# Attention and mixture-of-experts layer on one core: keys of a block turned by transposing DMAs, and the block cut into eight steps

## The chip, the cores and the metric

The kernel runs on one core of a Trainium2 chip. A core has a matrix engine (TensorE, PE in the profile; its weight loads are PEld), a vector engine (VectorE, DVE), a scalar engine (ScalarE, ACT), GpSimd (POOL) and a queue engine (SyncE, SP) that issues DMAs; 16 DMA engines move data between HBM and the on-chip memory SBUF, or within SBUF. Matmuls write to PSUM. The engines run side by side, each through its own instructions in order, and wait for one another on semaphores. The metric is device time in microseconds of one execution, as a median over runs.

## The reference

An input x of 8 sequences of 1024 tokens with 256 features is normalised (layer norm without gain) to xn, and two branches are added to x:

```python
q, k, v = (xn @ W.T).reshape(B, L, 16, 16)         # 16 heads of 16
q, k = elu(q) + 1, elu(k) + 1
kv_cumsum = cumsum(einsum('blhd,blhe->blhde', k, v), axis=1)
k_cumsum  = cumsum(k, axis=1)
out   = einsum('blhd,blhde->blhe', q, kv_cumsum)
denom = clip(einsum('blhd,blhd->blh', q, k_cumsum), 1e-6)
attn  = (out / denom).reshape(B, L, 256) @ Wo.T

logits = xn @ Wr + br                              # 8 experts, the best two per token
h   = silu(xn @ W1[e]) * (xn @ W3[e])              # 256 -> 512
ffn = sum over the two of weight * (h @ W2[e])     # 512 -> 256
result = x + attn + ffn
```

All of it is float32.

## The kernel before

**Two streams of work.** The FFN branch gathers tokens by expert into tiles of 128 rows. Tiles j = 0 to 131 are worked off in a loop (`tile_step`, L1397); each needs the expert's W1 and W3 (two DMAs of 512 KB from SP, `ffn_weights`, L1284, issued for tile j + 2 in step j into a ring of five buffers), 32 matmul records into `gu_ps` (L1310), a silu on ACT (L1318), a product `hT` on DVE (L1321), 8 matmul records into `y_ps` (L1329, for the tile before) and a scaling `y` on DVE (L1336), and a scattering DMA from POOL (L1340). The tiles 0 to 24 come from a first batch of lists, the others from a second, whose lists are made in tiles 12 to 21 (`second_batch`, L719: pieces of a one-hot on DVE, scalings on ACT, matmuls `held_ps` on PE).

The attention branch goes through 16 blocks of 512 tokens, two to a sequence, as a chain of steps (`block_steps`, L1032). It is linear attention in chunks of 128 tokens with a running state per head. A block t has nine steps:

1. q for both halves of the heads (`project_q`, elu, and masked copies qm by ACT, L829)
2. k of all four chunks (`project_k`, L841; elu by ACT, table load included, L786 and L787, and DVE, L789), with tokens on the partitions (`kn`)
3. k turned, so that features are on the partitions (`kT`): for each half of the heads four PE transposes (L882) and an ACT copy from PSUM (L885); then on DVE a running sum over the tokens (`ksum`, L887), its last column kept for the next block (`upto_t`, L891), and the product with q (L892)
4. v (`project_v`, four ACT copies L852) and the denominators: matmuls `den` (L904) from both products, clip and reciprocal on DVE (L910, L911), and eight DMAs from SP that spread the result (`rden`, L916)
5. the fetch of the next block's turned xn, the scores of chunk 0 (`scores`, L928: PE L936, causal mask on DVE L943), and the output projection left over from the block before (`attend`, L1008)
6. to 9. one chunk each: `carry` (L955), scores of the next chunk, `weigh` (L973, L983; DVE L990, L993, L1002), and the projection of the chunk before.

**What sets the order.** In the main loop PE's instructions stand in the order in which the code issues them (`manual_schedule`, L1480). In a tile that is: attention's step or steps, gu of this tile, y of the tile before. The order on ACT, DVE and POOL is a planner's, except for instructions under `in_order`, which keep the program's order among themselves; SP's DMAs are all of that kind. How many attention steps have been made by tile j is a table (`upto`, L1456 to L1461); `attend_upto` (L1072) makes one step per tile, or two where the second is in `TOGETHER`, and may put a block's last step behind gu. The first ones of block 0 are made before the loop, with transposes on PE.

**Turning by DMA** is there already for the FFN: from tile 27 on the gathered rows xg are split by DVE into planes of their low and high 16-bit halves (`ffn_halves`, L1241), turned by a transposing DMA of two-byte elements (`ffn_turn_halves`, L1250, on SP between the two weight loads), and put together again by an ACT copy that interleaves the halves (`ffn_join`, L1259). Tiles before 27 are turned by PE (L1269, copy L1271).

**Buffers.** Pool `one` holds one buffer each of qT, qm, kn, kT and rden; `f_x` holds five buffers of 4 KB per partition for blocks of x, loaded for blocks 4 to 15; `ps_mm` is a ring of four PSUM banks shared by gu, projections and scores, `ps_y` one of two shared by y, den and a.

Of the kernel before, what the change touches and what calls it, by code (L numbers as in the profile page):

```python
# [46 lines left out]
F32 = mybir.dt.float32  # L47
I32 = mybir.dt.int32
BF16 = mybir.dt.bfloat16
U16 = mybir.dt.uint16  # L50
AF = mybir.ActivationFunctionType
ALU = mybir.AluOpType
AX = mybir.AxisListType

P = 128
# [9 lines left out]
def tile_attention_moe(  # L65
# [14 lines left out]
    nc = tc.nc  # L80
# [727 lines left out]
    def begin(t):  # L808
        names = dict(
            qT=[KC, TB], qm=[KC, 2, TB], kn=[NCH, H], kT=[KC, TB], rden=[NCH, KC, P]  # L810
        )
        tiles = {n: one.tile([P, *d], F32, tag=n, name=n) for n, d in names.items()}
        blocks[t] = tiles["qT"], tiles["qm"], tiles["kT"], tiles["kn"], va, tiles["rden"]
# [34 lines left out]
    def project_v(t, c):  # L848
# [6 lines left out]
            )  # L855
        yield

    def project(t):


        if t > 0:
            begin(t)
            for o in range(KC):
                for _ in project_q(t, o):
                    pass
                mask_q(t, o)
                yield
            for c in range(0, NCH, 2):
                for _ in project_k(t, c):
                    pass  # L870
                yield
        else:
            for _ in range(4):
                yield
        qT, qm, kT, kn, va, rden = blocks[t]
        upto_t = two.tile([P, KC], F32, tag="upto_t", name="upto_t")
        fresh = t % BLK_PER_SEQ == 0
        qks = []
        for o in range(KC):
            tp = ps_t.tile([P, TB], F32, tag="t", name="tp")  # L880
            for c in range(NCH):
                nc.tensor.transpose(  # L882
                    tp[:, bass.ts(c, P)], kn[:, c, bass.ts(o, P)], ident
                )
            nc.scalar.copy(kT[:, o, :], tp)  # L885
            ksum = two.tile([P, TB], F32, tag="ksum", name="ksum")
            nc.vector.tensor_tensor_scan(  # L887
                ksum, ones[:, 0:1].to_broadcast([P, TB]), kT[:, o, :],
                0.0 if fresh else sums[0][:, o : o + 1], ALU.mult, ALU.add,
            )  # L890
            nc.vector.tensor_copy(upto_t[:, o : o + 1], ksum[:, TB - 1 : TB])  # L891
            nc.vector.tensor_tensor(ksum, qT[:, o, :], ksum, ALU.mult)  # L892
            qks.append(ksum)
            yield
        for c in range(0, NCH, 2):
            if t > 0:
                for _ in project_v(t, c):
                    pass
            yield

        den = ps_y.tile([P, P], F32, tag="y", name="den")
        for o in range(KC):
            for c in range(NCH):
                nc.tensor.matmul(  # L904
                    den[32 * c : 32 * c + 32, :], lhsT=own_of[:, o, :],
                    rhs=qks[o][:, bass.ts(c, P)], start=(o == 0), stop=(o == KC - 1),
                    skip_group_check=True,
                )
        over = one.tile([P, P], F32, tag="over", name="over")
        nc.vector.tensor_scalar(over, den, EPS_DEN, None, ALU.max)  # L910
        last_masked[0] = nc.vector.reciprocal(over, over)  # L911
        for c in range(NCH):
            for o in range(KC):
                heads_of = slice(32 * c + HALF * o, 32 * c + HALF * (o + 1))
                in_order(
                    nc.sync.dma_start(  # L916
                        out=rden[:, c, o, :],
                        in_=over[heads_of, :].unsqueeze(1).to_broadcast([HALF, HD, P]),
                    )
                )  # L920
        yield
        del xnTs[t]
        sums[0] = upto_t

# [107 lines left out]
    def block_steps(t):  # L1032


        for i, _ in enumerate(project(t)):
            if i in (1, 3, 5, 8):
                yield
        if t + 1 < NBLK:
            fetch(t + 1)
        waiting = scores(t, 0)  # L1040
        if behind:
            attend(*behind.pop())
        yield
        done = None
        for c in range(NCH):
            if done:
                attend(*done)
            both_ps = carry(t, c)
            coming = scores(t, c + 1) if c + 1 < NCH else None
            oT = weigh(both_ps, *waiting)  # L1050
            done = t, c, oT
            waiting = coming
            yield
        behind.append(done)
        if t + 1 == NBLK:
            attend(*behind.pop())
            yield

    STEPS = 9
    LAST = NBLK * STEPS + 1  # L1060

    TOGETHER = (0, 4, 8)
    steps_made = [0]

    def attention():
# [325 lines left out]
    LATE = 3  # L1391
    LISTS = NBLK - FB
    READ = LISTS + 10
    AHEAD = 2 + LISTS // 2 + 3 * (READ - LISTS) // 2
    held = {}

    def tile_step(j):  # L1397
# [58 lines left out]
        if j < LISTS:  # L1456
            upto = 3 + j // 2
        elif j < READ:
            upto = AHEAD - 3 * (READ - j - 1) // 2
        else:  # L1460
            upto = AHEAD + (LAST - 1 - AHEAD) * (j - READ + 1) // (NM - 1 - READ) + j // (NM - 1)  # L1461
        waits = attend_upto(upto, put_off=True)
# [74 lines left out]
```

## Time and profile before

| | |
|---|---|
| median of 3 runs | 1265.2 us (1262.7 to 1265.59) |
| profiled execution | 1257.66 us, span 1255.5 us |
| PE busy | 1205.5 us, 96% |
| DVE, ACT, POOL busy | 675.3, 554.5, 527.9 us |
| transposes of k, L882 | 128 records, 273 ns median each, overlapping |
| copies of kT on ACT, L885 | 32, 586 ns median |
| key sums, L887 with a carried start | 16, 1266 ns median |
| transposing DMAs, L1250 | 105, issue 1227 ns median |
| joins of halves, L1259 | 105, 757 ns median |
| DMA in total | 245.84 MB, mean 196 GB/s |

A line of the timeline reads: start in us, length in us, engine, line of the kernel, operation, output<-input, shapes, number of instructions merged; in brackets the idle time of that engine before it and who ended it. Merged matmuls overlap, so what a group costs PE is read from its start to the next group's start. A line of the windows view gives a stretch, its length, the busy time of PE, PEld, DVE, ACT and POOL (instructions in brackets), the granted TensorE clock as a share of full speed, the DMA engines' mean busy share and GB/s.

### The profile page before, as it was taken

What the parts mean: (1) busy time and instruction counts of PE and PEld (TensorE: products, weight loads), DVE (VectorE), ACT (ScalarE), POOL (GpSimd) and SP (SyncE); (2) the same over time, 40 slices, a digit from 0 to 9 for tenths busy, and PEclk for the clock granted to TensorE, in tenths of its full rate; (3) what the DMA queues carried; (4) which work ended last, traced back from release to release, by engine and by line L of the source; (5) the groups of instructions that cost most, each with busy time, mean ns of one, the idle gap of its engine ahead of it and who ended that gap; (6) DMA issues with size and microseconds to landing.
All of it is one profiled execution on the core that took longest, in us unless ns stands there. A gap on an engine that the chain in (4) does not pass through costs nothing.

```text
span 1255.5 us, 29756 instructions
## 1 busy us (share of the span) xinstructions
PE 1205.5 (96%) x11460; PEld 1059.7 (84%) x11460; DVE 675.3 (54%) x1541; ACT 554.5 (44%) x1064; POOL 527.9 (42%) x460
## 2 busy tenths in 40 slices
PE   7788898999999999999999999999999999999994
PEld 5677787888888889888888889989888889898884
DVE  7776669975344544545453545445453545445451
ACT  5665454471624335262625335262626243352610
POOL 4733234325443544444434544444443354444322
PEclk8899999999999999999999999999999999999997
DMA  9788565747987887969888787979897987879672
GB/s 339 274 276 266 150 209 116 237 115 229 245 196 182 193 198 167 244 151 227 177 200 182 187 202 167 223 169 223 185 200 171 189 193 178 205 165 247 145 178 33
DMA packets 203934, 245.84 MB, mean 196 GB/s; under 512 B 72946, under 2 KB 127858, under 8 KB 203506
## 3 DMA queue, kind: packets, MB, share of 16 engines
q1 hardware_dynamic: 161010, 191.79, 52.9%
q0 software_dynamic: 38032, 43.22, 24.6%
q10 hardware_dynamic: 4752, 8.91, 2.0%
q8 instruction: 94, 1.54, 0.5%
q14 instruction: 46, 0.38, 0.1%
HBM read 187.91 MB, written 44.29 MB: 185 GB/s over the span
## 4 chain that ended last, share of the span: by engine, by line
PE 87%; DVE 7%; DMA 2%; ACT 2%; issue 1%; SPq 0%; POOL 0%; POOLq 0%; ACTq 0%; DVEq 0%
PE gu_ps L1310 36%; PE y_ps L1329 17%; PE s_ps L936 5%; PE o_ps L973 5%; PE a_ps L1015 5%; PE zq L819 4%; PE zkk L835 4%; PE zkv L835 4%; PE o_ps L955 2%; DMA xb<-in_x_dram 1%; PE tp L882 1%; PE held_ps L749 1%; PE tp L358 1%; PE den L904 1%; DVE st L312 1%
## 5 line engine op out<-in xcount | busy, mean ns | idle before, releaser
L1310 PE MATMUL gu_ps<-xgT,w 128*128 128x128 f32 x4224 | 504.6, 277 | 6.4 <-issue 2.9
L1310 PEld LDWEIGHTS gu_ps<-xgT,w 128*128 128x128 f32 x4224 | 487.3, 192 | 21.1 <-issue 12.7
L1340 POOL DMA_INDIRECT out_dram<-y,dst_i x107 | 175.4, 1639 | 320.2 <-DVE y L1336 96.8
L1329 PE MATMUL y_ps<-w_sb,hT 128*128 x1056 | 250.9, 380 | 2.1 <-DVE tab L327 1.1
L1218 POOL DMA_INDIRECT xg<-in_x_dram,src_i x132 | 129.0, 977 | 229.1 <-DVE half L1241 114.4
L1329 PEld LDWEIGHTS y_ps<-w_sb,hT 128*128 128x128 f32 x1056 | 190.5, 190 | 24.8 <-issue 1.6
L1318 ACT ACTIVATE hT<-gu_ps 128x512 f32<-128x512 f32 x132 | 78.8, 597 | 286.9 <-PE gu_ps L1310 237.4
L943 DVE TENSOR_TENSOR s_sb<-s_ps,causal 128x512 f32<-128x512 f32 x256 | 159.0, 681 | 70.5 <-PE s_ps L936 68.1
L1321 DVE TENSOR_TENSOR hT<-gu_ps,hT 128x512 f32<-128x512 f32 x132 | 90.3, 684 | 63.0 <-PE gu_ps L1310 28.2
L1223 POOL DMA_INDIRECT entry<-tab_d,of_i x107 | 107.2, 1002 | 39.5 <-issue 31.4
L1336 DVE TENSOR_SCALAR y<-y_ps,entry 128x256 f32<-128x256 f32 x132 | 63.7, 482 | 109.9 <-PE y_ps L1329 109.9
L1241 DVE COPY half<-xg 128x512 uint16<-128x512 uint16 x105 | 47.9, 457 | 130.7 <-ACT xg L1231 130.7
L1020 ACT COPY at<-a_ps 128x256 f32<-128x256 f32 x64 | 23.8, 373 | 173.0 <-PE a_ps L1015 123.0
L1259 ACT COPY xgT<-halfT 128x512 uint16<-128x512 uint16 x105 | 79.7, 759 | 5.1 <-DMA halfT<-half 5.1
L1231 ACT ACTIVATE xg<-xg,entry 128x256 f32<-128x256 f32 x132 | 78.4, 595 | 2.1 <-DMA entry<-tab_d,num_i 2.1
L936 PE MATMUL s_ps<-qm,kT 32*128 32x256 f32 x1024 | 75.3, 400 | 0.1
L1015 PE MATMUL a_ps<-wo_sb,oT 128*128 128x256 f32 x256 | 67.9, 388 | 2.9 <-DVE y L1336 2.0
L973 PE MATMUL o_ps<-s_sb,va 128*32 128x128 f32 x2048 | 69.2, 276 | 0.0
L973 PEld LDWEIGHTS o_ps<-s_sb,va 128*32 128x32 f32 x2048 | 52.0, 109 | 17.8 <-issue 15.9
L1340 POOL DMA_INDIRECT acc_d<-y,src_i x25 | 44.2, 1766 | 52.6 <-DVE y L1336 23.3
L835 PE MATMUL zkv<-wkv_sb,xnT 128*128 128x256 f32 x256 | 59.9, 388 | 0.0
L835 PE MATMUL zkk<-wkv_sb,xnT 128*128 128x256 f32 x256 | 59.4, 386 | 0.0
(228 smaller groups left out, 1339.1 us busy)
## 6 DMA issues: line engine op xcount, KB each, us to landing
w<-in_w_dram SPq DMA_DIRECT2D x264, 512.0 KB
rden<-over SPq DMA_DIRECT2D x128, 64.0 KB
xnT<-xnT_d SPq DMA_DIRECT2D x15, 512.0 KB
out_dram<-at POOLq DMA_DIRECT2D x13, 512.0 KB
out_dram<-in_x_dram SPq DMA_DIRECT2D x12, 512.0 KB
xnT_d<-xnT ACTq DMA_DIRECT2D x11, 512.0 KB
xb<-in_x_dram SPq DMA_DIRECT2D x9, 512.0 KB
w_sb<-in_w_dram SPq DMA_DIRECT2D x4, 1024.0 KB
```

The source lines that it names most:

```text
L835: nc.tensor.matmul(z[:, i, :], lhsT=xnTs[t][:, k, bass.ts(c + i, P)], rhs=wkv_sb[:, k, a, :], start=(k == 0), stop=(k == KC - 1),)
L936: nc.tensor.matmul(s_ps[r][:, hh].rearrange("p a l -> p (a l)"), lhsT=kT[rows, hh, span], rhs=qm[rows, hh, :, span], start=True, stop=True,)
L943: last_masked[0] = nc.vector.tensor_tensor(sm, s_ps[r].rearrange("p k a l -> p (k a) l"), causal_b, ALU.mult)
L973: nc.tensor.matmul(o_ps[32 * r : 32 * r + 32, hh, :], lhsT=va[:, c, 4 * hh + r, a, :], rhs=s_sb[r][:, 2 * hh + a, :], start=(first and a = ...
L1015: nc.tensor.matmul(a_ps, lhsT=oT[:, hh, :], rhs=wo_sb[:, hh, :], start=(hh == 0), stop=(hh == 1),)
L1218: rows = nc.gpsimd.indirect_dma_start(out=xg[j], out_offset=None, in_=x_rows[:, :], in_offset=bass.IndirectOffsetOnAxis(ap=src_i[:, i : i ...
L1223: nc.gpsimd.indirect_dma_start(out=entry[j], out_offset=None, in_=table[:, :], in_offset=bass.IndirectOffsetOnAxis(ap=num_i[:, i : i + 1], ...
L1259: nc.scalar.copy(xgT[j].bitcast(U16).rearrange("p k (l b) -> p b k l", b=2), halves.pop(j).rearrange("p (b k) l -> p b k l", b=2),)
L1310: done = nc.tensor.matmul(ps[:, i, :], lhsT=w13[:, k, bass.ts(i, P)], rhs=xgT[j][:, k, :], start=(k == 0), stop=(k == KC - 1),)
L1321: nc.vector.tensor_tensor(hT, gu[1], hT, ALU.mult)
L1329: done = nc.tensor.matmul(y_ps, lhsT=hT[:, i, :], rhs=w2_sb[:, bass.ds(e * (IC * H) + i * H, H)], start=(i == 0), stop=(i == IC - 1),)
L1340: nc.gpsimd.indirect_dma_start(out=rows[:, :], out_offset=bass.IndirectOffsetOnAxis(ap=dst_i[:, i : i + 1], axis=0), in_=ys.pop(j), in_off ...
```

## The change

From block 1 on k is turned in the way that xg is. `planes` takes two buffers of `f_x` per block: DVE copies kn into planes of 16-bit halves (two copies of 1024 two-byte elements per partition), SP issues four transposing DMAs, one per chunk, and ACT joins the halves into kT (two copies, one per half of the heads, 1024 two-byte elements each). PE's eight transposes and ACT's two copies from PSUM go, in blocks 1 to 15; block 0 keeps them.

The steps of a block are now eight: k with the split into halves; the four transposing DMAs and q; v, then the joins and the key sums (`key_sums`, as before on DVE); denominators together with the next fetch, the scores of chunk 0 and the left-over projection; four chunks. `TOGETHER` and the table of steps per tile follow: from tile 12 on one step per tile.

```diff
+    key_state = {}
+
+    def key_sums(t, o):
+
+        qT, kT = blocks[t][0], blocks[t][2]
+        upto_t, qks = key_state[t]
+        ksum = two.tile([P, TB], F32, tag="ksum", name="ksum")
+        nc.vector.tensor_tensor_scan(
+            ksum, ones[:, 0:1].to_broadcast([P, TB]), kT[:, o, :],
+            0.0 if t % BLK_PER_SEQ == 0 else sums[0][:, o : o + 1], ALU.mult, ALU.add,
+        )
+        nc.vector.tensor_copy(upto_t[:, o : o + 1], ksum[:, TB - 1 : TB])
+        nc.vector.tensor_tensor(ksum, qT[:, o, :], ksum, ALU.mult)
+        qks.append(ksum)
+
+    def planes(name):
+
+        tile_ = f_x.tile([P, NCH, H], F32, tag="xb", name=name)
+        return tile_.rearrange("p c h -> p (c h)").bitcast(U16)
+
     def project(t):
 
 
+        key_state[t] = two.tile([P, KC], F32, tag="upto_t", name="upto_t"), []
         if t > 0:
             begin(t)
+            kT, kn = blocks[t][2:4]
+            halves_k = planes("k_half").rearrange("p (c b h) -> p c b h", c=NCH, b=2)
+            for c in range(0, NCH, 2):
+                for _ in project_k(t, c):
+                    pass
+            for c in range(0, NCH, 2):
+                nc.vector.tensor_copy(
+                    halves_k[:, c : c + 2],
+                    kn[:, c : c + 2].bitcast(U16).rearrange("p c (h b) -> p c b h", b=2),
+                )
+            yield
+            turned_k = planes("k_halfT").rearrange("p (b o l) -> p b o l", b=2, o=KC)
+            for c in range(NCH):
+                in_order(
+                    nc.sync.dma_start_transpose(
+                        out=turned_k.rearrange("p b o l -> p (b o) l")[:, :, bass.ts(c, P)],
+                        in_=halves_k[:, c].rearrange("p b h -> p (b h)"),
+                    )
+                )
             for o in range(KC):
                 for _ in project_q(t, o):
                     pass
                 mask_q(t, o)
-                yield
+            yield
             for c in range(0, NCH, 2):
-                for _ in project_k(t, c):
-                    pass
-                yield
-        else:
-            for _ in range(4):
-                yield
...
+                for _ in project_v(t, c):
                     pass
+            for o in range(KC):
+                in_order(
+                    nc.scalar.copy(
+                        kT[:, o].bitcast(U16).rearrange("p (l b) -> p b l", b=2),
+                        turned_k[:, :, o],
+                    )
+                )
+                key_sums(t, o)
             yield
-
+        else:
+            kT, kn = blocks[t][2:4]
+            yield
+            yield
...
+    def denominators(t):
+
+        rden = blocks[t][5]
+        upto_t, qks = key_state.pop(t)
         den = ps_y.tile([P, P], F32, tag="y", name="den")
...
     def block_steps(t):
 
 
-        for i, _ in enumerate(project(t)):
-            if i in (1, 3, 5, 8):
-                yield
+        yield from project(t)
+        denominators(t)
         if t + 1 < NBLK:
             fetch(t + 1)
         waiting = scores(t, 0)
...
-    STEPS = 9
+    STEPS = 8
     LAST = NBLK * STEPS + 1
 
-    TOGETHER = (0, 4, 8)
+    TOGETHER = (0, 7)
...
-    AHEAD = 2 + LISTS // 2 + 3 * (READ - LISTS) // 2
+    AHEAD = 2 + LISTS // 2 + READ - LISTS
...
-            upto = AHEAD - 3 * (READ - j - 1) // 2
+            upto = AHEAD - (READ - j - 1)
```

More of the change, by code (lines that the diff above doesn't have):

```diff
@@ L866, in project @@
                 mask_q(t, o)
-                yield
+            yield
             for c in range(0, NCH, 2):
-                for _ in project_k(t, c):
-                    pass
-                yield
-        else:
-            for _ in range(4):
-                yield
[L875 to L893, printed above, removed]
-            yield
-        for c in range(0, NCH, 2):
-            if t > 0:
                 for _ in project_v(t, c):
                     pass
-            yield
+            for o in range(KC):
[6 more added lines that the diff above has]
+                key_sums(t, o)
+            yield
+        else:
+            kT, kn = blocks[t][2:4]
+            yield
+            yield
+            for o in range(KC):
+                tp = ps_t.tile([P, TB], F32, tag="t", name="tp")
+                for c in range(NCH):
+                    nc.tensor.transpose(
+                        tp[:, bass.ts(c, P)], kn[:, c, bass.ts(o, P)], ident
+                    )
+                nc.scalar.copy(kT[:, o, :], tp)
+                key_sums(t, o)
+            yield
+    def denominators(t):
+        rden = blocks[t][5]
+        upto_t, qks = key_state.pop(t)
         den = ps_y.tile([P, P], F32, tag="y", name="den")
@@ L920, in project @@
                 )
-        yield
         del xnTs[t]
@@ L1032, in block_steps @@
     def block_steps(t):
-        for i, _ in enumerate(project(t)):
-            if i in (1, 3, 5, 8):
-                yield
+        yield from project(t)
+        denominators(t)
         if t + 1 < NBLK:
```

## The prediction

> **What bounds the kernel now.** I read the page first: busy shares and the 40 slices.
>
> ```profile
> span 1255.5 us, 29756 instructions
> ...
> PE 1205.5 (96%) x11460; PEld 1059.7 (84%) x11460; DVE 675.3 (54%) x1541; ACT 554.5 (44%) x1064; POOL 527.9 (42%) x460
> ...
> PE   7788898999999999999999999999999999999994
> ```
>
> TensorE is busy 96% of the span, and from slice 10 on it does not pause. Second, the windows view: the stretch in which the second batch's lists are made (tiles 13 to 20), and the steady part after it.
>
> ```profile
> 182.20:283.10 100.90, 93.75 (x860) 81.28 (x860) 90.56 (x208) 55.61 (x188) 32.34 (x21) 0.98 0.55 158
> 337.00:1230.00 893.00, 892.90 (x8576) 793.26 (x8575) 437.56 (x807) 377.18 (x637) 384.93 (x315) 1.00 0.84 190
> ```
>
> Columns: length, busy us of PE, PEld, DVE, ACT, POOL, granted clock, DMA share, GB/s. In the steady 893 us PE idles 0.1 us: a microsecond of PE work saved there is one won, and a wait that PE gains is one lost. In the list stretch DVE is at 90%, so it binds there almost as much as PE.
>
> Third, the timeline of one block, because the change rebuilds its order. Each FFN tile is on PE [one attention step] [gu] [y of the tile before].
>
> ```profile
> 901.69 1.04 PE L882 MATMUL tp<-ident,kn 128*128 128x128 f32 x8
> 902.56 3.74 PE L1310 MATMUL gu_ps<-xgT,w 128*128 128x128 f32 x32
> 906.13 1.89 PE L1329 MATMUL y_ps<-w_sb,hT 128*128 x8
> 907.86 3.62 PE L835 MATMUL zkv<-wkv_sb,xnT 128*128 128x256 f32 x16
> 911.41 0.64 PE L904 MATMUL den<-ksum,own_of 128*32 128x128 f32 x16
> ...
> 902.32 1.07 ACT L885 COPY kT<-tp 128x512 f32<-128x512 f32 x2 [0.45 <-PE tp L882]
> ...
> 911.52 0.65 ACT L852 COPY va<-zkv 128x256 f32<-128x256 f32 x2 [1.08 <-PE zkv L835]
> ...
> 902.94 2.46 DVE L887 TENSOR_TENSOR_SCAN ksum<-ones,upto_t,kT 128x512 f32<-128x512 f32 x2 [0.22 <-ACT kT L885]
> 905.32 0.27 DVE L891 COPY upto_t<-ksum 128x1 f32<-128x1 f32 x2
> 905.51 1.28 DVE L892 TENSOR_TENSOR ksum<-qT,ksum 128x512 f32<-128x512 f32 x2
> 906.71 0.58 DVE L1241 COPY half<-xg 128x512 uint16<-128x512 uint16 x1
> 907.22 0.67 DVE L1321 TENSOR_TENSOR hT<-gu_ps,hT 128x512 f32<-128x512 f32 x1
> ```
>
> See the slack: the key sums (L887 to L892) begin at 902.94, as soon as kT is there, end at 906.79, and their reader, den, starts at 911.41. A whole tile, zkv included, lies between: 4.6 us of cover.
>
> **What goes.** The eight transposes of blocks 1 to 15: start to start 902.56 - 901.69 = 0.87 us of PE time, in a stretch without gaps. 15 x 0.87 = **13.0 us won**. The two kT copies of ACT (588 ns each) go as well; ACT has room (44%).
>
> As to a rule: the Trainium skill, page "VectorE: DVE Perf Modes", section "The three transpose paths", gives 390 ns for a 128x128 transpose on TensorE, 1309 ns by DMA, and its rules advise TensorE. By 390 ns the change would win 15 x 8 x 0.39 = 46.8 us; the trace's 0.87 us for eight decides.
>
> **What comes, on covered resources.** Two DVE copies per block into halves, 1024 two-byte elements each: L1241 takes 457 ns for 512, so 0.46 to 0.91; I take 0.85, 1.7 us in the k tile. There ACT's chain of L786/L787 sets the pace and DVE is busy 2.73 of 6.17 us (896.39 to 902.56); uncovered it would be 1.7 us per block. Four transposes on SP: L1250 issues in 1.21 to 1.25 us, so 4.9 us per block. They stand behind tile j+2's weights and ahead of j+3's; SP there waits for PE anyway (L1289 waited 406.6 us in 177 times for gu), and the weights are wanted two tiles later. What queues behind is the next halfT transpose, about 2 us late, whose reader follows a tile later. If the cover fails, the price is the rival on DMA below. Bytes: 60 x 128 KB = 7.9 MB on 245.8, a 0.84 share becoming some 0.87.
>
> Merging den with the first scores, and seven steps around them, moves PE work between tiles but leaves its sum; with PE gapless that costs nothing unless a step waits for its operands. One does.
>
> **What comes on the path: den.** In the built order of the changed kernel, k, q and v have a tile each; ACT turns the halves into kT only behind v's four copies, and den is the first PE work of the next tile. So the chain that began a whole tile ahead of den now begins after zkv, with gu and y alone as cover. With zkv's start as 0, from the rows above:
> - PE reaches den after zkv, gu and y. gu to y is 906.13 - 902.56 = 3.57, y to zkv 1.73, and the k tile, with the same work as v's, takes 8.76 (gu at 887.63 to gu at 896.39), so zkv is 3.46: den at 8.76, its second half (the other eight heads' sums; den takes 911.98 - 911.41 = 0.57) at 9.05.
> - ACT ends the v copies at 911.52 + 0.65 - 907.86 = 4.3. Then the two joins. No row has this form; the same copy with 512 elements (L1259) takes 757 ns, so 1024 take between 1.19 (plus 0.43, the step from 373 to 588 ns in ACT's copies of 256 and 512) and 1.52 (twice). I take 1.30, nearer the slope, as part of 757 is fixed. The first join ends at 5.6.
> - DVE's order from there, in blocks 3 to 15 alike: scan 1.23, upto 0.14, product 0.64, scan 1.23, the FFN's hT 0.67, upto 0.14, the FFN's half 0.43, product 0.64 = 5.12. It ends at 10.75. Before, hT and half stood behind the sums or ahead of them with time to spare; now they stand between the second scan and its product, 1.1 us.
> - So PE waits 10.75 - 9.05 = 1.7 us for the second half; successive instructions overlap by some 0.05 to 0.1 us each, so I take **1.65**. With the ends of the join 1.5 to 1.95, and 1.4 if every overlap counts.
>
> Behind den wait scores, a_ps, gu: all shift with it. Net per block 1.65 - 0.87 = +0.78; blocks 3 to 15: 13 x 0.78 = **+10.1 us**.
>
> Block 2 (tile 22) is worse. Its FFN tiles still turn xg on PE, and ACT has the joins behind the FFN's xgT copy, which needs PE after gu (7.0 + 0.4) and is followed by xg (0.6): joins end near 9.5 and 10.7, and DVE has y (after 8.98) ahead of the sums. Sums end 9.65 + 1.23 + 0.14 + 0.64 + 1.23 + 0.14 + 0.64 = 13.7 against 9.3: wait 4.4, net +3.5, and a halved clock window behind it (below) 1.7 x 1/2: **+4.4**.
>
> Block 1 lies in the list stretch, where DVE is nearly full. The steps there fall from 15 to 10 in tiles 12 to 21, which shortens PE's work per tile and not DVE's list work (at_place 0.68, held 0.61, parts 0.33 us for each of 32 pieces). Before, PE idled 100.9 - 93.75 = 7.2 us there. Bounds: -7 (that idle time goes) to +7 (it doubles, as DVE is to fill shorter tiles); as DVE also gets block 2's and block 1's halves I take +3, less 0.87: **+2**.
>
> Sum: 10.1 + 4.4 + 2 = **+16.5 us**. The profiled execution took 1257.7 us (span 1255.5), so it would become 1274; the median of the runs is 1265.2, 7.5 above that execution, and I forecast for it: **1282 us**.
>
> **The clock.** A window of 3.41 us with PE busy for 1.55 was followed by half clock, one with 1.70 was not:
>
> ```profile
> 23.81:27.22 3.41, 1.55 (x19) 1.23 (x21) 3.08 (x11) 3.00 (x7) 0.00 (x0) 1.00 1.10 384
> 27.22:30.63 3.41, 3.41 (x22) 2.54 (x15) 3.07 (x13) 1.28 (x4) 1.20 (x3) 0.50 1.09 444
> 85.25:88.66 3.41, 1.70 (x15) 1.73 (x16) 3.31 (x12) 1.23 (x3) 2.14 (x2) 1.00 1.02 403
> 88.66:92.07 3.41, 3.41 (x43) 3.17 (x42) 3.41 (x17) 2.60 (x5) 0.47 (x1) 1.00 1.07 380
> ```
>
> So idle time of 1.7 is let pass and 1.86 is not; half clock for 3.41 us costs 1.7 us of work. A wait of 1.65 stays just under it. The page "TensorE: Matmul & The Clock Gate", section "Why this matters for your kernels", warns only of gaps over some 3 us; by it these waits would never cost clock, and this rival would be nothing. The rows are stricter.
>
> **Rivals.**
> 1. *Faster: den does not wait.* If joins and sums end by 9.05, only the 13.0 us remain: 1252. For: kT's copies before waited for PE alone (7.3 us in 17). Against: 5.12 us of DVE behind a first join that can't end before 5.5. It decides where the wait falls under 0.87, half of what I find. 0.12; waits of 0.6 to 1.1 with early blocks at their low end give no change: 0.06.
> 2. *Clock.* If the join is at its upper end, waits of 1.95 halve the clock where they fall in one window, about (3.41 - 1.95 + 0.2)/3.41 = half of 13 blocks: 7 x 1.7 = 12, and 13 x 0.3 = 4 for the longer wait: 1282 + 16 = 1298. 0.16.
> 3. *DMA.* Four transposes in a row, each waiting for its halves, hold up SP: one in the trace took 3.27 us to issue against 1.23. Four such are 13 us, past the join's 4.3 in the v tile by about 3: 15 x 3 = 45 on top, 1327. Against: of 105 xgT joins only three waited, 5.1 us in all. 0.06.
>
> **Numbers.** Forecast with its own range 1270 to 1292 (13 x +-0.3, early blocks +-6): 0.60. Faster cases 0.12, no change 0.06, slower 0.82, where 0.3% (3.8 us) is about what this measurement can tell. The range leaves out the faster rival and the DMA one: 1264 to 1304.
>
> **What would show it.** Right: no transposes on PE in blocks 1 to 15; idle before den, ended by the product of the key sums, 13 times 1.4 to 1.95 us, and two longer ones; zero PE gaps in the other tiles; joins of 1.2 to 1.5 us. Wrong: den starting with no gap; joins waiting for DMA; PEclk below 1.00 after den; PE gaps in the k or q tile (ACT late with silu or masks).

## The result, and the profile after

| | before | after |
|---|---|---|
| median | 1261.9 us (6 runs, 1259.12 to 1265.59) | 1272.8 us (6 runs, 1271.56 to 1274.85) |
| ratio | | 1.0085, 95% interval 1.0065 to 1.0104 |
| profiled execution, span | 1257.66, 1255.5 us | 1272.69, 1270.9 us |
| PE busy, granted clock | 1205.5 us, 0.987 | 1196.4 us, 0.985 |

The change makes the kernel slower by 0.85%, about 11 us. One thing is needed to read the numbers further down: under the conditions of most experiments the kernel before took 1287 us and the changed one 1297, and the profiles taken there, but not these two, show short pauses of TensorE (last section). Ratios are always to the kernel before, run beside the other under the same conditions; where the pauses weigh in, the text goes by lines of the profile.

The page of the changed kernel, busy shares and slices:

```profile
span 1270.9 us, 29684 instructions
...
PE 1196.4 (94%) x11340; PEld 1046.9 (82%) x11340; DVE 693.8 (55%) x1571; ACT 575.7 (45%) x1066; POOL 532.4 (42%) x460
...
PE   8689898998999999999999999999999999999994
...
PEclk9899998998999999999999999999999999999998
```

PE has 120 records fewer (15 x 8 transposes) and is busy for 9.1 us less, yet the span is 15.4 us longer: what was saved came back as idle time, 24.5 us of it. The windows view, over the two stretches that the prediction showed, says where (columns as there):

```profile
182.20:283.10 100.90, 92.21 (x820) 79.08 (x819) 89.22 (x217) 57.36 (x184) 35.12 (x23) 0.95 0.67 179
337.00:1230.00 893.00, 876.39 (x8369) 774.15 (x8368) 447.39 (x825) 398.28 (x643) 385.13 (x314) 1.00 0.89 198
```

In the steady 893 us PE idles for 16.6 us, against 0.1 before, at full clock. In the list stretch the clock is down to 0.95 (0.98 before). The view of waits (engine, line, whom it waited for: us in total, times, longest) names the steady loss at once:

```profile
PE den L941 <- DVE ksum L870: 20.6, 15, 2.6
PE gu_ps L1345 <- ACT xgT L1306: 4.3, 2, 3.8
PE held_ps L749 <- ACT parts L611: 3.2, 1, 3.2
PE held_ps L749 <- DVE parts L609: 3.1, 3, 2.0
```

Before, PE never waited for den. Now it does 15 times: 13 times for 1.20 to 1.38 us (mean 1.27), once in each of the blocks 3 to 15, and twice in block 2 (2.63 and 1.42 us). The timeline of one of the 13, from v to the first scores:

```profile
502.45 3.62 PE L835 MATMUL zkv<-wkv_sb,xnT 128*128 128x256 f32 x16
...
505.90 3.73 PE L1345 MATMUL gu_ps<-xgT,w 128*128 128x128 f32 x32
506.10 0.65 ACT L852 COPY va<-zkv 128x256 f32<-128x256 f32 x2 [0.78 <-PE zkv L835]
506.63 2.56 ACT L913 COPY kT<-k_halfT 128x1024 uint16<-128x1024 uint16 x2
508.02 1.28 DVE L865 TENSOR_TENSOR_SCAN ksum<-ones,upto_t,kT 128x512 f32<-128x512 f32 x1 [2.78 <-ACT kT L913]
...
509.47 1.89 PE L1364 MATMUL y_ps<-w_sb,hT 128*128 x8
509.53 0.69 DVE L870 TENSOR_TENSOR ksum<-qT,ksum 128x512 f32<-128x512 f32 x1
...
510.14 1.28 DVE L865 TENSOR_TENSOR_SCAN ksum<-ones,upto_t,kT 128x512 f32<-128x512 f32 x1
...
511.29 0.42 PE L941 MATMUL den<-ksum,own_of 128*32 128x128 f32 x8
511.33 0.67 DVE L1356 TENSOR_TENSOR hT<-gu_ps,hT 128x512 f32<-128x512 f32 x1
511.92 0.14 DVE L869 COPY upto_t<-ksum 128x1 f32<-128x1 f32 x1
511.98 0.42 DVE L1276 COPY half<-xg 128x512 uint16<-128x512 uint16 x1
512.31 0.68 DVE L870 TENSOR_TENSOR ksum<-qT,ksum 128x512 f32<-128x512 f32 x1
...
513.04 0.43 PE L941 MATMUL den<-ksum,own_of 128*32 128x128 f32 x8 [1.33 <-DVE ksum L870]
```

Read it from the bottom: den's second half starts 0.05 us after the second product of the key sums ends; that product stands on DVE behind the FFN's hT and half, these behind the second scan, the scans behind the joins (L913), the joins on ACT behind v's four copies (L852), and these behind zkv. One chain from zkv to den, with gu and y as PE's only work beside it. What PE loses is a little more than the idle time shown, because the modelled ends of the first half's matmuls reach into the gap. Taken from start to start, den costs PE 26.8 us behind 330 us where it cost 7.5 before: 19.3 us in 13 blocks, **1.48 us** each, against 0.88 us of transposes (L882: 11.4 us in 13 blocks) that are gone. Net +0.61 per block, +7.9 us of the 15.4 between the two profiles.

The other 7.5 us lie in the first 330 us, by the starts of the tiles between tile 12 and tile 30: this stretch takes 192.4 us where it took 187.5, although 2.6 us of work (16 records of den, 16 of scores, 4 of the projection) have moved behind it. Before tile 12 a comparison says little: gu's wait for the second tile's xgT, at some 60 us, lasts between 2.2 and 8.1 us over all profiles, 2.2 and 3.6 in two of the kernel before.

### The profile page after: what moved, and what is told of

It reads as the page before. It is cut to its first block, busy times and chain, and to the rows that moved or that the text cites. A ratio compares the mean times of both kernels' runs of the same rounds, so it can differ in the third digit from the quotient of the medians.

```text
span 1270.9 us, 29684 instructions
## 1 busy us (share of the span) xinstructions
PE 1196.4 (94%) x11340; PEld 1046.9 (82%) x11340; DVE 693.8 (55%) x1571; ACT 575.7 (45%) x1066; POOL 532.4 (42%) x460
## 3 DMA queue, kind: packets, MB, share of 16 engines
q8 instruction: 93, 1.52, 0.5%
## 4 chain that ended last, share of the span: by engine, by line
PE 78%; DVE 12%; ACT 4%; issue 3%; DMA 2%; POOL 0%; SPq 0%; ACTq 0%; DVEq 0%; POOLq 0%
PE gu_ps L1345 31%; PE y_ps L1364 15%; PE s_ps L972 5%; PE o_ps L1009 5%; PE a_ps L1051 5%; PE zkv L835 4%; PE zkk L835 4%; PE zq L819 4%; DVE ksum L865 3%; PE o_ps L991 2%; ACT kT L913 1%; DVE ksum L870 1%; DMA xb<-in_x_dram 1%; PE tp L358 1%; PE held_ps L749 1%
## 5 line engine op out<-in xcount | busy, mean ns | idle before, releaser
L1253 POOL DMA_INDIRECT xg<-in_x_dram,src_i x132 | 131.7, 998 | 205.9 <-DVE half L1276 79.9
L979 DVE TENSOR_TENSOR s_sb<-s_ps,causal 128x512 f32<-128x512 f32 x256 | 158.5, 680 | 67.1 <-PE s_ps L972 67.1
L1051 PEld LDWEIGHTS a_ps<-wo_sb,oT 128*128 128x128 f32 x256 | 47.3, 192 | 16.1 <-issue 5.0
```

The costliest lines, as they stand in the source:

```text
L979: last_masked[0] = nc.vector.tensor_tensor(sm, s_ps[r].rearrange("p k a l -> p (k a) l"), causal_b, ALU.mult)
L1051: nc.tensor.matmul(a_ps, lhsT=oT[:, hh, :], rhs=wo_sb[:, hh, :], start=(hh == 0), stop=(hh == 1),)
L1253: rows = nc.gpsimd.indirect_dma_start(out=xg[j], out_offset=None, in_=x_rows[:, :], in_offset=bass.IndirectOffsetOnAxis(ap=src_i[:, i : i ...
```

## The experiments

**The joins first.** ACT's joins and the key sums are issued ahead of v's copies in the same tile.

```diff
-            for c in range(0, NCH, 2):
-                for _ in project_v(t, c):
-                    pass
             for o in range(KC):
                 in_order(
                     nc.scalar.copy(
                         kT[:, o].bitcast(U16).rearrange("p (l b) -> p b l", b=2),
                         turned_k[:, :, o],
                     )
                 )
                 key_sums(t, o)
+            for c in range(0, NCH, 2):
+                for _ in project_v(t, c):
+                    pass
             yield
```

> The changed kernel with one thing moved: in a block's v step the two joins and the key sums are issued ahead of the v projection, so that from block 3 on ACT makes kT before it copies v, and DVE's sums begin some 2 us after the v tile's start instead of 5.6. Theory (den waits for joins and sums that begin behind v): the waits of 1.2 to 1.4 us in blocks 3 to 15 go, 13 x 1.27 = 16.5 us; the two waits of block 2 stay, as there the joins still stand behind the FFN's work; 1256 us, faster than the kernel before by some 0.4%. Rival (transposing DMAs that land late or load the DMA engines): the joins would wait for them all the earlier, no gain, 1272 us. Rival (the loss is that of the eight-step order in the list stretch, not of den): 1266 us or more.

> The kernel with the joins ahead of v once more. Its 0.9886 came from a call in which TensorE made pauses of 0.45 us in the carry's matmuls behind GpSimd's indirect loads (after: 25 pauses, L1019 19 us longer than without; this kernel: 5). Theory (its own gain is den's 19.2 us less the 11.0 us that gu now waits, the rest is pauses that it misses): where the kernel before takes 1262 us, ratio 1.002 to 1.004; where it takes 1287 us, 0.987 to 0.990 again. Rival (the gain is its own): 0.987 to 0.990 in either.

Measured: 1272.67 us, ratio 0.9886 (0.985 to 0.9922), and again 1273.98 us, 0.9916 (0.9886 to 0.9946), beside a kernel before of 1287 us both times, so that the second run only repeats the first. The waits of den in blocks 3 to 15 are gone. A new one stands a few microseconds behind them. The timeline of a block of the first of the two runs:

```profile
515.12 0.64 PE L941 MATMUL den<-ksum,own_of 128*32 128x128 f32 x16
515.22 0.48 DVE L1371 TENSOR_SCALAR y<-y_ps,entry 128x256 f32<-128x256 f32 x1
...
516.03 1.63 POOL L1375 DMA_INDIRECT out_dram<-y,dst_i  x1 [0.30 <-issue]
...
516.83 0.29 DVE L947 TENSOR_SCALAR over<-den 128x128 f32<-128x128 f32 x1 [1.12 <-PE s_ps L972]
517.16 0.95 DVE L948 RECIPROCAL over<-over 128x128 f32<-128x128 f32 x1
...
518.03 2.42 DVE L979 TENSOR_TENSOR s_sb<-s_ps,causal 128x512 f32<-128x512 f32 x4
...
518.76 3.81 PE L1345 MATMUL gu_ps<-xgT,w 128*128 128x128 f32 x32 [0.86 <-issue]
```

den is whole and early. But the first scores fill all four banks of `ps_mm`; gu needs one back, which DVE's first mask (L979) frees, and the mask stands behind over and the reciprocal. Here over begins 1.07 us after den's end, and gu starts 0.10 us after the first mask ends, 0.86 us late. In 11 of the 13 blocks it is so: over 0.97 to 1.13 us behind den, gu 0.76 to 0.92 us late. By lines, den gives back 19.3 us and gu's wait takes 10.7.

**Twice the transposing transfers.** Each block's four transposing DMAs are issued twice.

```diff
-            for c in range(NCH):
-                in_order(
-                    nc.sync.dma_start_transpose(
...
+            for _ in range(2):
+                for c in range(NCH):
+                    in_order(
+                        nc.sync.dma_start_transpose(
...
```

> The changed kernel with its four transposing DMAs per block issued twice, into the same tile: 120 instead of 60. Theory (SP's time and the DMA engines' share are covered, all 4.9 us on SP per block): 1273 us within 4 us, with the waits before den unchanged at 1.2 to 1.4 us. Rival (the transposes are what makes den late or hold up the weights): another 0.5 to 3 us in each of 15 blocks, 1280 to 1318 us, with joins that wait for DMA.

Measured: 1301.39 us, ratio 1.0118 (1.0084 to 1.0153); the waits of den are 1.20 to 1.33 us as with four transfers. Four more transfers per block, 4.9 us of SP's time, leave the steady blocks as they are, and no join waits for a transfer. In block 1, in the list stretch, den then waited too (1.74 and 2.29 us): the joins stand there on ACT behind more of the list's and the FFN's work than with four transfers. Tiles 13 to 20 take 5.4 us longer than in the changed kernel under the same conditions; 6.8 us less of pauses hide that in the ratio. In blocks 3 to 15 the transfers are covered, with room for as many again.

**The eight steps with k turned by PE.** The new order and table, but eight transposes and two copies from PSUM per block, as before, and the sums in the q step.

```diff
             yield
-            turned_k = planes("k_halfT").rearrange("p (b o l) -> p b o l", b=2, o=KC)
...
+            for o in range(KC):
+                tp = ps_t.tile([P, TB], F32, tag="t", name="tp")
+                for c in range(NCH):
+                    nc.tensor.transpose(
+                        tp[:, bass.ts(c, P)], kn[:, c, bass.ts(o, P)], ident
+                    )
+                nc.scalar.copy(kT[:, o, :], tp)
             for o in range(KC):
                 for _ in project_q(t, o):
                     pass
                 mask_q(t, o)
+                key_sums(t, o)
             yield
...
-                key_sums(t, o)
             yield
```

> The eight-step order alone: k, q, v, den with first scores, four chunks as in the changed kernel, but k is turned by PE at the start of the q tile, with ACT copies from PSUM, and the key sums are made there; no halves, no transposing DMAs, no joins. Theory: PE has its 13.0 us of transposes back, den waits nowhere (16.5 us in blocks 3 to 15, 4.0 us and a halved clock window of 1.7 us in block 2): 1273 + 13 - 22 = 1264 us, the kernel before within 4 us. Rival (the order itself costs in the list stretch or at other waits): 1268 us or more, with PE gaps outside den.

Measured: 1282.03 us, ratio 0.9959 (0.9933 to 0.9986). No wait of den behind 330 us: in steady blocks den's wait belongs to the DMA way. But the ratio isn't the worth of the order. This run has fewer of the pauses than the changed kernel (from tile 27 on the carry's line takes 19.6 us, 29.5 there). Tiles 12 to 30 take 195.8 us, against 192.4 in the changed kernel and 187.5 before; of that the carry's pauses are 5.3 us more than in the changed kernel, and a window of halved clock behind four of them makes gu 2.5 us longer. Without both they would take some 188 us (an estimate), about as long as before, with the 2.6 us of den, scores and projection left for later.

**The second scan made twice.** 1.28 us of DVE work more in the chain of blocks 1 to 15.

```diff
+        for _ in range(1 if t == 0 or o == 0 else 2):
             nc.vector.tensor_tensor_scan(
                 ksum, ones[:, 0:1].to_broadcast([P, TB]), kT[:, o, :],
...
```

> The changed kernel with the running sum of the second half of the heads made twice in blocks 1 to 15 (the same sum, written again): DVE's chain before den is 1.2 us longer per block. Theory: the wait before den becomes 2.5 us instead of 1.27 in 13 blocks, +16 us, and block 2 +1.2; and as idle time over some 1.86 us in one 3.41 us window halves the clock of the next, about two thirds of the 13 waits cost 1.7 us more, +15: 1304 us, PEclk 0.5 for a window behind many of them. By the rule that only gaps over some 3 us count (the page on the clock gate) the clock stays: 1290 us. Rival (den's wait is of no account): 1273 us.

Measured: 1325.82 us, ratio 1.0281 (1.0228 to 1.0333). The 13 waits are 2.44 to 2.64 us, so the whole of the scan's 1.28 us lands on PE: the wait follows the chain's length. den costs 44.2 us from start to start, 17.4 more than in the changed kernel, and 10 of the 13 waits are followed by half clock, which lengthens the scores and what follows them by 16 us. Two of its windows of 3.41 us with the window after each (length, then PE's busy time; the granted clock is the third number from the end):

```profile
383.03:386.44 3.41, 1.32 (x24) 0.88 (x24) 3.19 (x7) 0.00 (x0) 1.59 (x2) 1.00 0.37 115
386.44:389.85 3.41, 3.41 (x15) 2.89 (x12) 2.78 (x5) 0.37 (x1) 0.69 (x1) 0.50 0.35 66
526.39:529.80 3.41, 1.82 (x15) 1.11 (x13) 3.41 (x5) 0.84 (x2) 0.00 (x0) 1.00 0.82 280
529.80:533.21 3.41, 2.38 (x28) 1.56 (x28) 3.19 (x8) 0.00 (x0) 2.65 (x2) 1.00 0.30 77
```

The wait of 2.6 us costs clock where it falls into one window (1.32 us busy) and none where a window's edge divides it (1.82).

**The changed kernel again, under these conditions.**

> The changed kernel itself, as the mark for the three others of the same chip. Ratio to before 1.0085 by the first comparison; if the early part of the program or the chip makes the difference, it moves within 1.0065 to 1.0104.

Measured: 1297.05 us, ratio 1.0076 (1.0054 to 1.0098). The same waits, and block 2's of 3.28 and 1.39 us; in addition 22 pauses of TensorE in the carry's matmuls: from tile 27 on the carry takes 18.8 us longer than in the first profile.

**The FFN's hT and half behind the sums.** The products of the key sums and the FFN's hT are held in program order.

```diff
-        nc.vector.tensor_tensor(ksum, qT[:, o, :], ksum, ALU.mult)
+        in_order(nc.vector.tensor_tensor(ksum, qT[:, o, :], ksum, ALU.mult))
...
-        nc.vector.tensor_tensor(hT, gu[1], hT, ALU.mult)
+        in_order(nc.vector.tensor_tensor(hT, gu[1], hT, ALU.mult))
```

> Theory (the wait of den's second half is the whole chain, and the FFN's hT and half, which stand between the second scan and its product on DVE, are part of it): with both behind the product, the product starts some 0.2 us behind the scan, as the first half's does, in place of 0.89 us; 13 waits of 1.27 fall to about 0.6, 13 x 0.65 = 8.5 us less than after, ratio to before 1.0085 - 0.0067 = 1.002. Rival (the wait is set by the joins on ACT alone, the FFN's instructions fit into idle time): waits of 1.2 to 1.4 as before, ratio 1.0085. A third case: hT comes later and PE then waits for it at y (waits at y of 0.3 or more per block), ratio 1.006 or more.

Measured: 1301.24 us, ratio 1.0095 (1.0061 to 1.0128). The theory was right on the wait (0.54 to 0.67 us) and wrong on the time. The timeline shows why:

```profile
590.62 0.69 DVE L870 TENSOR_TENSOR ksum<-qT,ksum 128x512 f32<-128x512 f32 x1
591.23 0.69 DVE L1356 TENSOR_TENSOR hT<-gu_ps,hT 128x512 f32<-128x512 f32 x1
591.37 0.42 PE L941 MATMUL den<-ksum,own_of 128*32 128x128 f32 x8 [0.56 <-DVE ksum L870]
591.72 1.37 PE L972 MATMUL s_ps<-qm,kT 32*128 32x256 f32 x16
...
593.75 2.42 DVE L979 TENSOR_TENSOR s_sb<-s_ps,causal 128x512 f32<-128x512 f32 x4
594.48 2.69 PE L1345 MATMUL gu_ps<-xgT,w 128*128 128x128 f32 x22 [0.32 <-issue]
```

hT reads gu's second bank, and the scores need that bank: put behind the sums it ends at 591.92, and the scores take 1.30 us where they take 1.08; then half, y, over and the reciprocal push the first mask back, and gu waits for its bank (0.32 us). Of den's 8.6 us, scores and gu's wait take back 3.0 and 5.3: nearly all of it.

**den behind the scores.** One move on PE: den's matmuls after the first scores and the left-over projection.

```diff
-        denominators(t)
         if t + 1 < NBLK:
             fetch(t + 1)
         waiting = scores(t, 0)
         if behind:
             attend(*behind.pop())
+        denominators(t)
         yield
```

> The changed kernel with one move on TensorE: den's matmuls behind the first scores and the left-over projection in place of ahead of them, which gives the chain of joins and sums 1.08 + 0.98 = 2.1 us more cover, against a wait of 1.27. Theory (the wait is all that the steady blocks lose): no idle time before den in blocks 3 to 15, 13 x 1.27 = 16.5 us less, block 2's wait of 4.05 down to about 2 with less halved clock, 2 to 5 us less: 1272.8 - 16.5 - 3.5 = 1253, ratio to before 0.991 to 0.995. Rival (the reciprocal then comes too late: over and its eight DMAs start 2 us later, oT and what stands behind it on DVE wait for them, and PE waits at a_ps or at the next carry): 1.000 to 1.006.

Measured: 1279.96 us, ratio 0.9953 (0.9929 to 0.9976), at the edge of what the theory said; but the gain is not where it said. There is no wait of den in blocks 3 to 15, and behind 330 us no wait for a late reciprocal either. The scores, now first, meet hT: they take 1.76 us on average in place of 1.08, because hT stands on DVE behind the second scan and holds one of their four banks. 8.9 of den's 19.3 us go that way. In the early part 3.4 us are won in tiles 22 to 24 and 4.2 lost in tiles 12 to 22, where a_ps waits 3.19 us for an oT that stands on DVE behind the list work.

The four kernels side by side, all with the pauses, as TensorE's time by line from each record's start to the next one's, from the first gu of tile 27 to the end, so that all four have the same work in it:

| line | after | joins first | hT behind sums | den behind scores |
|---|---|---|---|---|
| den | 26.7 | 7.5 | 18.1 | 7.5 |
| scores | 55.9 | 55.9 | 59.0 | 64.8 |
| a_ps, with gu's wait behind it | 48.0 | 58.7 | 53.4 | 48.3 |
| gu | 383.6 | 383.3 | 385.4 | 384.2 |
| carry (L1019), with the pauses | 29.5 | 13.9 | 28.2 | 17.2 |
| all lines, against after | | -24.4 | -0.1 | -20.8 |
| the same without the carry | | -8.9 | +1.1 | -8.5 |
| start of tile 27, against after | | +1.7 | +5.1 | +5.2 |

The last row, the early part, goes on top of the first sum; together they come within 2 us of the medians (-24.4, +4.2, -17.1). So some 60% of what two of the kernels win over the changed one in these lines is pauses that they miss (15.6 of 24.4 us, 12.3 of 20.8). Without the pauses the joins first would win 7 to 9 us on the changed kernel, an estimate: its lines without the carry are 8.9 us less than the changed kernel's here and 6.8 less than in the changed kernel's first profile. That would be a ratio of 1.0015 to 1.003 to the kernel before, so no gain. It wasn't measured without them.

**Blocks 1 and 2 by PE.** Blocks 1 and 2 as in the run with k turned by PE; the rest as changed, or, in the second run, with the joins first.

```diff
+            if t > 2:
                 kT, kn = blocks[t][2:4]
                 halves_k = planes("k_half").rearrange("p (c b h) -> p c b h", c=NCH, b=2)
...
+            else:
+                kT, kn = blocks[t][2:4]
...
+                    for c in range(NCH):
+                        nc.tensor.transpose(
+                            tp[:, bass.ts(c, P)], kn[:, c, bass.ts(o, P)], ident
+                        )
+                    nc.scalar.copy(kT[:, o, :], tp)
...
```

> Theory (about 10 of after's 10.9 us lie in blocks 1 and 2: the joins behind the FFN's copies on ACT, den's 4.05 us wait with halved clock, and waits in the list stretch; not in the eight steps): with blocks 1 and 2 turned by PE and the rest as in after, no den wait in blocks 1 and 2, the 13 steady waits unchanged at 1.2 to 1.4, and a net cost of 13 x (1.27 - 0.87) = 5.2 us over the variant that turns all blocks by PE (0.9959): ratio 1.000. Rival (the early loss is the new table of steps): only 2 x 0.87 us more PE work against den's wait, ratio 1.006 to 1.008.

> Blocks 1 and 2 turned by PE, blocks 3 to 15 by DMA with the joins and key sums ahead of v. Theory: the gain of the joins first (0.9886) less the early loss that is left in it (den's 3.27 + 1.39 us wait of block 2 with two halved windows, 3.4 us of work lost, and waits in the list stretch), plus 1.7 us for the transposes of two blocks: 0.980 to 0.985. Rival (the early loss is the table of steps): 0.988 to 0.990.

Measured: 1298.93 us, ratio 1.0083 (1.0053 to 1.0112); with the joins first 1271.0 us, 0.987 (0.9837 to 0.9902). By the medians the theory falls: block 2's wait is gone, yet the kernel isn't faster than the changed one beside it (1.0076). The starts of the tiles show more. Against the changed kernel 6.2 us are won from tile 22 to 24, where block 2's wait was; 1.9 are lost from 12 to 22, where the transposes of the two blocks take 2.2; 2.5 are lost from 24 to 30 and 2.5 behind them, and there the carry's pauses take 2.6 and 2.6 us more. Without the pauses some 4 us would be left as the gain (an estimate): less than the theory's 10, more than the 2 at most of the rival. The view of waits has `held_ps` at 4.4 us where the changed kernel has 3.2, though no transfer is made there. The second kernel has the lowest median under these conditions, 1.3% below the one before, but the intervals don't tell it from the joins first. Its carry takes 23.7 us in the whole run against 16.1 in the changed kernel without pauses, so that its span of 1268.9 would be near 1261 without them (an estimate), and the kernel before has 1255.5 and 1260.8.

**The kernel before, profiled for itself; more steps in the list stretch.** 13 in place of 10 steps in tiles 12 to 21.

```diff
-    AHEAD = 2 + LISTS // 2 + READ - LISTS
+    AHEAD = 2 + LISTS // 2 + 13 * (READ - LISTS) // 10
...
-            upto = AHEAD - (READ - j - 1)
+            upto = AHEAD - 13 * (READ - j - 1) // 10
```

> The kernel before with its profile on the chip of the experiments, where it takes 1287 in place of 1262 us. Theory (this chip adds pauses of some 0.45 us within the carry's matmuls, L983 here, when GpSimd has begun an indirect load, L1218 or L1223, within the microsecond before; the kernels before and after have them alike): 35 to 55 pauses, 16 to 24 us in all, PE without gaps elsewhere behind 330 us, and those in which a load has begun are hit, the others not. Rival (everything on this chip runs slower): matmuls and copies longer throughout, no pauses.

> The changed kernel with 13 in place of 10 attention steps in tiles 12 to 21, which brings it about as far by tile 22 as the kernel before (21 of 129 steps against 23 of 145; after: 18). Theory (the early loss is the table: PE's work per tile shortened against unchanged list work on DVE, so that PE idles): PE's gaps between 185 and 330 us fall from 15.7 to about 10 and the time by about 5 us, ratio 1.0076 - 0.004 = 1.0035. Rival (the early loss is the way over DMA in blocks 1 and 2, wherever it falls): gaps as before or longer, since block 2's joins now meet the list work, ratio 1.007 to 1.010.

These two ran without the pauses: the kernel before took 1262.44 us again (ratio 1.0004, 0.9986 to 1.0022) with three short waits behind 330 us, so neither theory nor rival on its 1287 us is tested. The longer table: 1279.27 us, ratio 1.014 (1.0121 to 1.016), slower than the changed kernel. The theory falls. The first wait in the list stretch stays at 3.21 us, and block 2's den now waits 4.69 + 1.39 us, with the clock halved for 10.2 us. That is what the rival said, and costs more than it said: block 2's joins meet the list work, on ACT, where they stand behind eight scalings (L611) that wait for `held_ps`. The view of waits:

```profile
PE den L941 <- DVE ksum L870: 22.7, 15, 4.7
PE held_ps L749 <- ACT parts L611: 3.4, 2, 3.2
```

## Why the prediction was right, point by point

The sign, the place and the mechanism held, and 1272.8 lies in its range of 1264 to 1304. The forecast of 1282 was 9 us too high. One sign was missed by a little: the 13 idle times before den were to be 1.4 to 1.95 us long, and are 1.20 to 1.38.

- **The 13.0 us won** were won: 0.88 us per block from start to start, and no transposes are left in blocks 1 to 15. The 390 ns that the prediction quotes from the Trainium skill stand there for bf16 elements; these are float32, and eight in a row cost 0.11 us each.
- **den's wait** of 1.65 us was 1.48 from start to start (1.27 as idle time). With zkv's start as 0 the chain of the block shown reads: v's copies end at 4.30 (4.3 forecast), the first scan starts at 5.57 (5.6), den at 8.84 (8.76), the sums end at 10.54 (10.75). The join takes 1.355 us (1.30 taken). The largest term that was off is DVE's sequence of eight instructions, 4.97 us in place of 5.12: the overlaps that the prediction named were larger than the 0.05 it took off. Then den's start, 0.08 late. 13 x 0.61 = 7.9 us, not 10.1.
- **Block 2** waited for 4.05 us (4.4 forecast), but the clock stayed halved for two windows, not for one:

```profile
294.69:298.10 3.41, 0.78 (x8) 0.35 (x10) 2.60 (x5) 2.29 (x2) 2.62 (x2) 1.00 0.68 265
298.10:301.51 3.41, 1.99 (x24) 1.09 (x28) 2.53 (x5) 0.00 (x0) 1.49 (x2) 0.50 0.37 39
301.51:304.92 3.41, 3.41 (x18) 2.33 (x15) 2.72 (x5) 0.13 (x1) 0.00 (x0) 0.50 0.18 25
```

  The second part of the wait (1.42 us) falls into the halved window, which is then busy for 1.99 us, and the next is halved as well.
- **The list stretch** got the sign and reason forecast (shorter tiles against the same list work): PE's first wait for `held_ps` is 3.21 us where it was 1.93, and three windows are at half clock (192.28 for 6.8 us, 209.35 for 3.4) where one was. The first line is of the kernel before, the second of both kernels in which blocks 1 and 2 are turned by PE in the new order; the changed kernel's stands with the result:

```profile
PE held_ps L749 <- ACT parts L611: 2.8, 2, 1.9
PE held_ps L749 <- ACT parts L611: 4.4, 1, 4.4
```

  So these waits belong to the eight steps and not to the way over DMA. Blocks 1 and 2 and the list stretch together cost 7.5 us net, 6.4 forecast. Some 4 of them went when blocks 1 and 2 were turned by PE (an estimate, pauses taken off), which is block 2's part (4.4 forecast); some 3.5 stayed, where the forecast took +2. That +2 was a choice between -7 and +7, so its nearness is in part luck. More steps in that stretch didn't mend it. Which of the moves in the new order makes it wasn't isolated and stays open.
- **The sum** was +16.5; the two profiled executions differ by 15.0 us, the medians by 10.9. before's profiled execution lay 4.2 us below its median and after's at its median, which accounts for the gap between these two; against the second profile of the kernel before, span 1260.8, the difference is 10.1. The forecast also started from the median of three runs, 1265.2; with six it is 1261.9.
- **The clock** beside the steady waits stayed full, as forecast: the windows around the waits are busy for 2.08 us or more. The run with the second scan doubled shows what the clock rival would have been, and that its price was real: 10 of 13 waits halved the clock. "TensorE: Matmul & The Clock Gate", section "Why this matters for your kernels", of the Trainium skill warns of gaps over some 3 us; waits of 2.44 to 2.64 us did it here where they fell into one window, so the rows were the better guide.
- **The DMA rival** fell: twice the transfers leave the waits of blocks 3 to 15 as they are. **The faster rival** fell with the first timeline: the sums end 1.4 us after PE is ready for them. The halves' copies took 0.69 us each (0.85 taken) and stayed covered.

## What to carry to other kernels

When work is taken off the engine that has no idle time, ask what now ends last ahead of its next instruction that needs the result: a whole tile of cover that is cut to a part of one turned 0.88 us saved into 1.48 us lost. Here no single move took the stall away for nothing: of the 19.3, 8.6 and 19.3 us that den gave back in three of them, 10.7, 8.3 and 8.9 were lost again to the next holder, a PSUM bank that hT or a mask had to free. So count the buffers as well as the engines. And when two kernels are compared, look at TensorE's time by line: a ratio alone had hidden that some 60% of an apparent gain was pauses that had nothing to do with the edit's purpose, and that another edit's gain of some 4 us was lost to them. Such a sum by line must cover the same tiles in both kernels: a cut at the same time of both takes in a tile more of the later one.

## What was not expected of the hardware

**Pauses of TensorE behind GpSimd's indirect loads.** In the profiles taken where the kernel before took 1287 us, PE paused for about 0.45 us (the median idle time shown), mostly once or twice, within the 16 short matmuls of the carry. From start to start a pause costs more: 18.8 us for the changed kernel's 22. The view of waits of the changed kernel there, and then its timeline around one pause:

```profile
PE o_ps L1019 <- issue: 9.3, 22, 0.7
```

Before the pause a gather's issue runs on GpSimd; the carry stops after seven matmuls and goes on 0.46 us later:

```profile
536.00 0.95 POOL L1253 DMA_INDIRECT xg<-in_x_dram,src_i  x1 [0.30 <-issue]
536.45 0.22 PEld L1019 LDWEIGHTS o_ps<-va,kn 128*32 128x32 f32 x3
536.56 0.58 PE L1019 MATMUL o_ps<-va,kn 128*32 128x32 f32 x7
536.88 0.15 PEld L1019 LDWEIGHTS o_ps<-va,kn 128*32 128x32 f32 x4 [0.21 <-issue]
537.59 0.21 PEld L1019 LDWEIGHTS o_ps<-va,kn 128*32 128x32 f32 x9 [0.56 <-issue]
537.61 0.31 PE L1019 MATMUL o_ps<-va,kn 128*32 128x32 f32 x9 [0.46 <-issue]
```

Over the ten profiles taken under that condition, the carry of a chunk behind 330 us paused (an idle time of over 0.15 us within it) in 72 of 89 cases in which GpSimd had begun an indirect load (the gathers of xg or of its entries) within the microsecond before, and in 23 of 383 in which it had not. In the four profiles without it, 0 of 49 such cases paused. When a gather starts follows from when DVE frees its buffer, so an edit on ACT or DVE shifts the gathers against the carry: with the joins first only 2 and 4 cases fell together, against 15 in the changed kernel. That is shown as a coincidence in time; why a load's issue should hold PE, and why under one condition alone, isn't settled.

**The clock's windows.** Over the changed kernel and the one with the doubled scan, from 60 to 1230 us, every window of 3.41 us at full clock with PE busy for 1.46 us or less was followed by half clock, every one with 1.66 or more was not, and of two at 1.51 and 1.52 one was. A window already halved needs more: all up to 3.22 us busy were followed by another halved one, those busy throughout were not.

**over's late start.** With the joins first, over began about 1 us after den's end in 11 of 13 blocks. It needs den alone; the view names the scores' end as what it waited for, but in five of these blocks it began before any score had ended. In those blocks GpSimd's gather issue ended just as y did, and another indirect issue, in ten of them a scatter's, began some 0.8 us ahead of over; where over got ahead of that scatter (the blocks at 863 and 1210 us, and all with k turned by PE) it was 0.07 to 0.29 us. In the changed kernel a gather's issue runs across over's start, and over comes 0.07 us behind den all the same. Whether the two engines hold each other up there was not tried.
